# A dilated 7x7 convolution in two-dimensional point evaluation, local attention and group whitening on one core: interpolating column points in pairs, evaluating the last row point by column points, and whitening in 64x64 parts

## The chip, the core and the metric

The kernel runs on one core of one Trainium2 chip. The metric is the device time of one launch in microseconds; the figure for a kernel is the median of several runs. The engines are PE (TensorE, matrix products), DVE (VectorE), ACT (ScalarE), POOL (GpSimd) and SP (SyncE, which here issues most DMAs). Matrix products go to PSUM, from where DVE or ACT take them to SBUF.

## The reference

The input is x, 4 images of 256 channels of 64 x 64 in float32. The first layer computes 49 attention maps by a 7x7 convolution with dilation 2 (256 to 128 channels), a 1x1 convolution to 49, and a softmax over the 49; the result of the layer is, at each pixel, the sum of the 49 shifted inputs weighted by these maps. The second layer whitens 4 groups of 64 channels each over all images and pixels, with five steps of a Newton iteration, and applies a gain and a shift per channel.

```
k = lax.conv_general_dilated(x, w1, window_strides=(1, 1), padding=[(6, 6), (6, 6)], rhs_dilation=(2, 2), ...) + b1
k = lax.conv_general_dilated(k, w2, ...) + b2
attn = jax.nn.softmax(k, axis=1)
shifts = jnp.stack([xp[:, :, 2*u:2*u+H, 2*v:2*v+W] for u in range(7) for v in range(7)], axis=1)
y = jnp.einsum('bkchw,bkhw->bchw', shifts, attn)
...
Sigma = EPS * I + jnp.einsum('gdm,gem->gde', xc, xc) / m
for _ in range(T_ITERS):
    P3 = jnp.einsum('gij,gjk,gkl->gil', P, P, P)
    P = 1.5 * P - 0.5 * jnp.einsum('gij,gjk->gik', P3, Sigma_N)
xn = jnp.einsum('gde,gem->gdm', P * jnp.sqrt(rTr), xc)
```

## The kernel before

**Convolution.** The two convolutions are folded into one of 256 to 49 channels at the start. It is then computed by polynomial evaluation and interpolation, in rows and in columns: of the rows of an image, row_eval makes a linear combination for each row point (0 to 5, and a point called INF); of each of those, col_eval makes one for each column point (xh). At each pair of points PE multiplies by weights that were evaluated in the same way (conv_bank, L502), for the two halves h of the columns side by side in PSUM. The column points come in three banks, (1, 2, 0), (3, 4, INF) and (5). A point has two taps, INF has one. After each bank ACT moves the products to the buffer pv (L512). When all three banks of a row point are there, col_interp turns them into that row point's values in zz, in 22 DVE instructions (L300, L303, L307), and when all row points of an image are there, row_interp turns zz into the 49 maps, in two parts of 17 and 5 instructions. The last row point of an image, 5, is treated in two parts also in col_interp. row_interp's second part and the first of the next image's operations are put in a written order on DVE (`in_order`).

**The row point INF** is not evaluated by column points before: it is one tap, and `direct` (L608) computes it as an ordinary convolution along the columns, 28 matrix products of about 496 columns, each two records in the trace. Row points 0, 4 and 5 of image 0 are direct too. `direct_inf` loads its weights (wi) from DRAM for images 1 to 3. Weights of a row point are evaluated once (`weights`), stored to DRAM (gd) and loaded for later images on SP's queue (wr).

**Attention** of an image lies between the banks of the following ones. Its steps for a quarter of an image are transposes of the maps and of the input (L926), band loads and stores (sd, band), stream transposes on DVE (L908), the weighted sums on PE (L955) whose outcome ACT brings to the slot (L974), turns back (L987) and the moments for whitening (L1008). The list `todo` holds what is due at each of eight gaps of an image; a gap comes when the costs of the banks so far (6, 5 and 2 per row point, 12 for the direct INF) reach the next eighth. The scheduler then orders each engine's instructions; before the first bank of image 1 (`strict`) and in `in_order` blocks DVE's order is the written one.

**Whitening.** At the end each 128 x 128 matrix wm (two groups of 64 on its diagonal) multiplies slots of 512 columns (L1276), and ACT (L1287) and DVE (L1291) by turns scale and shift the product into out, which goes to DRAM in stores of 512 KB with four buffers.

## Time and profile before

| what | us |
|---|---|
| median of 3 runs | 766.35 (765.34 to 767.47) |
| profiled execution, its own time | 765.48 |
| its span in the profile | 763.7 |
| PE busy | 716.1 (94%) |
| DVE busy | 623.9 (82%) |
| ACT busy | 325.9 (43%) |
| POOL busy | 34.2 (4%) |
| products at row and column points, L502 | 251.0 |
| direct row points, L608 | 34.8 |
| weighted sums, L955 | 154.8 |
| PE in the last 59.7 us, the apply of the whitening (L1276) | 55.02 |

The mean granted clock of PE was 0.982 of full speed. An engine's busy time sums the instructions of the profile; the span is what one execution takes from first to last instruction, and about 1.8 us of the profiled time lie outside of it. A group's line names the line of the kernel, the engine, the operation, the buffers (out from in), the shape, the count, and after the bar busy time and mean ns. Idle time ahead of an engine's instruction is put down to what ended it. One matrix product in float32 is two records.

### The profile page before, as it was taken

How to read it: one execution, taken by the hardware profiler on the slowest of the kernel's cores; microseconds unless marked ns; L12 is line 12 of the kernel's file. 1: busy time of each engine (PE TensorE's matmuls, PEld its weight loads, DVE VectorE, ACT ScalarE, POOL GpSimd, SP SyncE). 2: the span in 40 equal slices, each digit the busy share in tenths (PEclk: the TensorE clock that was granted, in tenths of full speed). 3: DMA queues.
4: the chain of work that ended last, by engine and by line, in shares of the span. 5: the costliest groups of instructions: out<-in, count | busy, mean ns of one | idle time of the engine just before them, and what ended most of it. 6: DMA issues, size and time to landing. Idle time of an engine off the chain costs nothing.

```text
span 763.7 us, 18389 instructions
## 1 busy us (share of the span) xinstructions
PE 716.1 (94%) x7444; PEld 545.6 (71%) x7444; DVE 623.9 (82%) x1302; ACT 325.9 (43%) x950; POOL 34.2 (4%) x46
## 2 busy tenths in 40 slices
PE   7999999789899999989999999998999889998997
PEld 1459643376798885979988948897998678775443
DVE  3799999999899999979995999699979665435443
ACT  2414240127544652665435435625535653332443
POOL 0510000300000010001000100000000000000000
PEclk9999999999899999999999999999999999998999
DMA  8991110054453672165545710443422143380776
GB/s 330 245 310 71 64 61 20 33 161 130 128 174 130 230 249 64 51 241 193 172 118 219 231 44 24 144 128 121 138 69 87 45 144 103 110 346 4 293 307 280
DMA packets 59773, 114.76 MB, mean 150 GB/s; under 512 B 22903, under 2 KB 42024, under 8 KB 58920
## 3 DMA queue, kind: packets, MB, share of 16 engines
q1 hardware_dynamic: 55992, 94.71, 37.1%
q0 software_dynamic: 3696, 18.88, 7.3%
q8 instruction: 59, 0.97, 0.5%
q14 instruction: 26, 0.21, 0.1%
HBM read 66.23 MB, written 47.33 MB: 149 GB/s over the span
## 4 chain that ended last, share of the span: by engine, by line
PE 41%; DVE 36%; ACT 5%; issue 4%; DMA 2%; SPq 1%; DVEq 0%; ACTq 0%
PE y L955 12%; PE cv L502 10%; PE tp L1276 7%; DVE xh L307 4%; PE sig L1008 3%; PE tp L987 3%; PE tp L926 3%; DVE rb L307 3%; DVE pv L307 3%; DVE ct L307 3%; DVE zz L307 3%; DVE band L908 2%; DVE ct L300 2%; DVE pv L303 2%; PE cv L608 2%
## 5 line engine op out<-in xcount | busy, mean ns | idle before, releaser
L502 PE MATMUL cv<-xh,wr 128*49 128x128 f32 x4368 | 251.0, 276 | 7.6 <-DVE xh L300 5.6
L502 PEld LDWEIGHTS cv<-xh,wr 128*49 128x49 f32 x4368 | 244.9, 124 | 12.7 <-issue 8.2
L955 PE MATMUL y<-band,xb 128*128 128x224 f32 (+2 forms) x640 | 154.8, 382 | 13.3 <-ACT xb L934 8.1
L955 PEld LDWEIGHTS y<-band,xb 128*128 128x128 f32 x640 | 111.8, 197 | 35.6 <-ACT xb L934 10.4
L512 ACT COPY pv<-cv 113x486 f32<-113x486 f32 (+1 forms) x63 | 29.9, 476 | 77.7 <-PE cv L502 76.6
L974 ACT ACTIVATE slot<-y,pivot 128x512 f32<-128x512 f32 x53 | 36.7, 741 | 60.5 <-PE y L955 60.5
L995 ACT COPY yt<-tp 128x256 f32<-128x256 f32 x128 | 45.4, 378 | 35.1 <-PE tp L987 34.1
L926 PE MATMUL tp<-ident,slot 128*128 128x128 f32 x256 | 50.5, 300 | 6.6 <-ACT yt L995 6.6
L987 PE MATMUL tp<-ident,slot 128*128 128x128 f32 x256 | 51.8, 298 | 3.9 <-ACT xb L934 1.4
L908 DVE STREAM_TRANSPOSE band<-band 128x960 f32<-128x960 f32 (+1 forms) x48 | 50.9, 1060 | 3.9 <-DMA band<-sd 3.8
L987 PEld LDWEIGHTS tp<-ident,slot 128*128 128x128 f32 x256 | 41.4, 205 | 13.9 <-issue 4.5
L926 PEld LDWEIGHTS tp<-ident,slot 128*128 128x128 f32 x256 | 40.1, 206 | 14.0 <-ACT yt L995 8.5
L1291 DVE TENSOR_SCALAR out<-tp,scale,beta 128x512 f32<-128x512 f32 x32 | 25.9, 810 | 29.5 <-PE tp L1276 29.5
L857 ACT COPY zt<-d 32x112 f32<-32x112 f32 (+2 forms) x156 | 45.0, 288 | 1.7
L811 ACT ACTIVATE d<-tp,mx 128x49 f32<-128x49 f32 x128 | 37.0, 337 | 14.5 <-DVE mx L806 10.8
L1287 ACT ACTIVATE out<-tp,beta,scale 128x512 f32<-128x512 f32 x32 | 24.9, 777 | 32.0 <-PE tp L1276 32.0
L307 DVE SCALAR_TENSOR_TENSOR xh<-ct 128x512 f32<-128x512 f32 x42 | 27.8, 683 | 12.4 <-PE cv L502 12.2
L934 ACT COPY xb<-tp 128x256 f32<-128x256 f32 x87 | 30.5, 380 | 16.6 <-PE tp L926 16.0
L1008 PE MATMUL sig<-yt 128*64 128x65 f32 x1024 | 36.9, 225 | 0.0
L1008 PEld LDWEIGHTS sig<-yt 128*64 128x64 f32 x1024 | 32.5, 137 | 6.0 <-issue 4.5
L1276 PE MATMUL tp<-slot,PS 128*128 128x512 f32 x80 | 35.9, 593 | 0.0
L608 PE MATMUL cv<-slot,wi 128*49 128x496 f32 (+3 forms) x168 | 34.8, 571 | 0.0
(206 smaller groups left out, 985.6 us busy)
## 6 DMA issues: line engine op xcount, KB each, us to landing
out_dram<-out SPq DMA_DIRECT2D x32, 512.0 KB, 2.6
sd<-zt SPq DMA_DIRECT2D x16, 896.0 KB, 3.9
slot<-in_x_dram POOLq DMA_DIRECT2D x12, 1024.0 KB, 10.3
band<-sd SPq DMA_DIRECT2D x128, 84.0 KB, 2.1
wr<-gd SPq DMA_DIRECT2D x15, 588.0 KB, 4.0
wr<-gd SPq DMA_DIRECT2D x15, 490.0 KB, 3.5
spill<-slot POOLq DMA_DIRECT2D x3, 2048.0 KB, 8.2
back<-spill SPq DMA_DIRECT2D x3, 2048.0 KB, 8.0
```

The lines of the kernel that those rows point to most:

```text
L307: return in_turn(STT(o, a, f, b, ALU.mult, ALU.add))
L502: nc.tensor.matmul(cv[h * HB : h * HB + KT, k, sr : sr + n, sc : sc + n], wv[:, sc, sr, cc], xh[bc][:, :n, h * NCC + cc, :n], start=(j == ...
L608: nc.tensor.matmul(ps[h * HB : h * HB + KT, :, w0:w1_], w[v][:, cc], xs[:, :, cc, w0 + d : w1_ + d], start=(j == 0), stop=(j == len(order) ...
L811: nc.scalar.activation(d[:, h, i], lt[i // NI][:, i % NI, h, :KT], AF.Exp, bias=mx[:, i, h : h + 1], accum_out=s[:, h, i : i + 1],)
L857: ins = nc.scalar.copy(o, i)
L908: nc.vector.transpose(f, f)
L926: nc.tensor.transpose(t[:, cc * P : (cc + 1) * P], xt[:, cc, CR * m : CR * (m + 1), bass.ds(pc, SW, 2)], ident,)
L955: nc.tensor.matmul(ps[:, cc, q0 - half * HALF : q1 - half * HALF, :], xb[:, cc * P : (cc + 1) * P], rhs, start=(k == 0), stop=(k == len(PI ...
L987: nc.tensor.transpose(t[:, cc * P : (cc + 1) * P], yt[:, cc, CR * i : CR * (i + 1), bass.ds(pc, SW, 2)], ident,)
L995: nc.scalar.copy(yb.rearrange("p a g c -> p (a g) c")[:, :, :GW], t[:, :C].rearrange("p (e c) -> p e c", c=GW),)
L1008: nc.tensor.matmul(sig[g * GW : (g + 1) * GW, cc], yb[:, cc, g, :GW], yb[:, cc, g], start=(count[0] == 0 and cc == 0), stop=(count[0] == 4 ...
L1276: nc.tensor.matmul(t, wm[cc], slots[2 * b + pr][:, cc, q * TR : (q + 1) * TR, :].rearrange("p r w -> p (r w)"), start=True, stop=True,)
```

## The change

**Row point INF at column points.** ROWS now begins with INF, and images 2 and 3 have seven row points, all of them evaluated at column points; INF's weights have one tap and are half as wide (98 for 196). They are made from a kept copy in DRAM (kept[INF]) at image 2 and loaded at image 3. Image 0's INF stays direct; image 1's also stays direct, but moves from behind that image's first row point to the end of the written prologue. The tile wi, its load and direct_inf go, and so do the two zi buffers, whose place zz has now (one plane more).

**Pairs.** col_interp takes two row points at once, (INF, 0), (1, 2) and (3, 4), in instructions of 113 x 324 in place of 113 x 162; pv is one tensor with three places for row points. Where the two places aren't neighbours in order (distance -2), two of the instructions are split. Row point 5, row point 0 of image 1 and row point 3 of image 0 stay single. The sum that part 1 needs goes to a plane of the products, no longer to a temporary.

**Prologue and costs.** The prologue's order changes with the pairs, and a bank's cost is scaled by its taps; there is no step of 12 for INF.

**Whitening.** The apply takes two blocks q of 512 columns together. For the first of the two column parities each is a product of 128 x 128 as before; the second parity is four of 64 x 64, two that write the partitions of their own group and two that write those of the other (ts[1]). The exchanged ones are brought back by two 64-partition moves, with scale and shift exchanged too (abx, made by one more product with a swap matrix). Products of 64 x 64 alternate between a pair of banks of ps_y and cv_buf; out has six buffers.

```
...
-ROWS = (0, 1, 2, 3, 4, 5)
+ROWS = (INF, 0, 1, 2, 3, 4, 5)
+PAIRS = ((INF, 0), (1, 2), (3, 4))
+AT = {br: k for k, br in enumerate(ROWS)}
...
-    zz = apool.tile([P, NP - 1, Q9, W], F32, name="zz")
-    zi = [apool.tile([P, Q9, W], F32, name=f"zi{k}") for k in range(2)]
-    for k in range(2):
-        nc.gpsimd.memset(zi[k], 0.0)
+    zz = apool.tile([P, NP, Q9, W], F32, name="zz")
+    nc.gpsimd.memset(zz[:, AT[INF]], 0.0)
+    NV = 3
+    pv = apool.tile([P, NP, NV, Q9, 2 * Q9], F32, name="pv")
...
-    it = ct.rearrange("p a b -> p (a b)")[:, :PT].rearrange("p (q b) -> p q b", q=Q9)
...
-    gd = [dram.tile([P, nsl, NSK], F32, name=f"gd{b}") for b in range(NP - 1)]
+    gd = [
+        dram.tile([P, nsl, NSK * len(taps(b)) // 2], F32, name=f"gd{b}") for b in range(NP)
+    ]
...
+    kept[INF] = dram.tile([P, KS * NSK // 2], F32, name="gi")
+    nc.sync.dma_start(kept[INF], tap[:, UPOS[3]].rearrange("p v a k -> p (v a k)"))
...
-        wt = apool.tile([P, ns, NSK], F32, tag=f"wr{i}", name=f"wr_{b}_{br}_{i}")
+        nk = NSK * len(taps(br)) // 2
+        wt = apool.tile([P, ns, NSK], F32, tag=f"wr{i}", name=f"wr_{b}_{br}_{i}")[:, :, :nk]
...
-            f = rb[0].rearrange("p q r c w -> p (q r c w)")[:, : KS * NSK]
+            f = rb[0].rearrange("p q r c w -> p (q r c w)")[:, : KS * nk]
...
-            f = f.rearrange("p (v a r k) -> p v a r k", v=KS, a=NCC, r=2)
+            f = f.rearrange("p (v a r k) -> p v a r k", v=KS, a=NCC, k=KT)
...
-            ct.rearrange("p a b -> p (a b)")[:, k * NSK : (k + 1) * NSK] for k in range(3)
+            ct.rearrange("p a b -> p (a b)")[:, k * nk : (k + 1) * nk] for k in range(3)
...
                 nc.scalar.copy(r[2], xs[:, 0])
+            elif br == INF:
+                nc.scalar.copy(r[1], xs[:, 3])
             for cc in range(NCC):
...
-        return rb[{1: 2, 2: 0, 3: 0, 4: 1, 5: 2, 0: 2}[br]]
+        return rb[{1: 2, 2: 0, 3: 0, 4: 1, 5: 2, 0: 2, INF: 1}[br]]
...
-    pvs = {}
+    slot = {}
...
-            pvs[b, br] = apool.tile(
-                [P, NP, Q9, 2 * Q9], F32, tag="pv", name=f"pv_{b}_{br}", bufs=2
-            )
+            slot[b, br] = len(slot) % NV
...
             nc.scalar.copy(
-                pvs[b, br][:K2, i0 : i0 + len(pts)].rearrange("p n q b -> p (n q b)"),
-                cv[:K2, : len(pts)].rearrange("p n q b two -> p (n q b two)"),
-            )
-    def interpolate(pt, tmp, outs, cut, part=None):
+                pv[:K2, i0 : i0 + len(pts), slot[b, br]].rearrange("p n q b -> p n (q b)"),
+                cv[:K2, : len(pts)].rearrange("p n q b two -> p n (q b two)"),
+            )
+    def interpolate(pt, tmp, outs, cut, part=None, each=lambda *a: (a,)):
...
             madd(tmp, s2, -16.0, tmp)
-            add(tmp, tmp, s4)
-            madd(outs[0], lo(s1), 1.0 / 6, hi(c0))
+            for o, x, y in each(outs[0], lo(s1), hi(c0)):
+                madd(o, x, 1.0 / 6, y)
             add(outs[2], lo(c6), hi(s3))
+            add(s3, tmp, s4)
         if part != 0:
-            madd(hh, tmp, -1.0 / 9, hh)
+            madd(hh, s3, -1.0 / 9, hh)
             madd(s4, hh, -3.0, s4)
...
             madd(s2, s4, -1.0 / 15, s2)
-            madd(outs[1], lo(s4), 1.0 / 15, hi(s2))
+            for o, x, y in each(outs[1], lo(s4), hi(s2)):
+                madd(o, x, 1.0 / 15, y)
     def phases(t):
-        return [t[:, :, bass.ds(4 + a - R if a < R else 0, Q8, 4)] for a in range(4)]
+        return [t[..., bass.ds(4 + a - R if a < R else 0, Q8, 4), :] for a in range(4)]
     def col_interp(b, br, part=None):
-        pv = pvs[b, br]
-        pt = {c: pv[:K2, i] for i, c in enumerate(ORDER)}
-        outs = phases(zz[:K2, br].rearrange("p q (w two) -> p q w two", two=2))
...
-        interpolate(pt, t[:K2], outs, cut, part)
+        brs = br if isinstance(br, tuple) else (br,)
+        s0, ds = slot[b, brs[0]], slot[b, brs[-1]] - slot[b, brs[0]]
+        v = pv[:K2, :, s0]
+        v = bass.AP(
+            tensor=v.tensor,
+            offset=v.offset,
+            ap=[list(v.ap[0]), [NV * PT, NP], [ds * PT, len(brs)], [2 * Q9, Q9], [1, 2 * Q9]],
+        )
+        pt = {c: v[:, i] for i, c in enumerate(ORDER)}
+        z = zz[:K2, AT[brs[0]] : AT[brs[0]] + len(brs)]
+        outs = phases(z.rearrange("p n q (w two) -> p n q w two", two=2))
+        cut = lambda t, k: t[:, :, :, 2 * k : 2 * (k + Q8)].rearrange(
+            "p n q (b two) -> p n q b two", two=2
+        )
+        t = ct.rearrange("p a b -> p (a b)")[:, : len(brs) * PT].rearrange(
+            "p (n q b) -> p n q b", q=Q9, n=len(brs)
+        )
+        each = lambda *a: (a,)
+        if ds not in (0, 1):
+            each = lambda *a: [[t[:, k] for t in a] for k in range(len(brs))]
+        interpolate(pt, t[:K2], outs, cut, part, each)
         if part != 0:
             nc.scalar.copy(outs[3], cut(pt[5], 0))
+        if INF in brs:
+            nc.gpsimd.memset(zz[:, AT[INF], Q8], 0.0)
     def row_interp(b, part):
-        pt = {k: zz[:K2, k] for k in range(NP - 1)}
-        pt[INF] = zi[b % 2][:K2]
+        pt = {k: zz[:K2, AT[k]] for k in range(NP)}
         lg = lgx
...
         lg = lg[:, : SH * W].rearrange("p (r w) -> p r w", w=W)
-        outs = [t[:, 0] for t in phases(lg[:K2].unsqueeze(1))]
+        outs = phases(lg[:K2])
         cut = lambda t, k: t[:, k : k + Q8]
-        tr = zi[(b + 1) % 2]
+        tr = ct.rearrange("p a b -> p (a b)")[:K2, : Q9 * W].rearrange("p (q w) -> p q w", w=W)
+        interpolate(pt, tr, outs, cut, part)
         if part == 0:
-            interpolate(pt, tr[:K2], outs, cut, 0)
             done_ = ((0, outs[0]), (2, outs[2]))
         else:
-            interpolate(pt, tr[:K2], outs, cut, 1)
-            nc.gpsimd.memset(tr[:, Q8], 0.0)
             done_ = ((3, cut(pt[5], 0)), (1, outs[1]))
...
-        z = zi[b % 2][:K2] if br == INF else zz[:K2, br]
+        z = zz[:K2, AT[br]]
...
-    gi = dram.tile([P, KS, NCC * KT], F32, name="gi")
-    nc.sync.dma_start(gi, tap[:, UPOS[3]].rearrange("p v a k -> p v (a k)"))
...
-    def direct_inf(b):
-        t = apool.tile([P, KS, NCC, KT], F32, tag="wi", name=f"wi_{b}")
-        nc.sync.dma_start(t.rearrange("p v a k -> p (v a k)"), gi.rearrange("p v k -> p (v k)"))
-        w = [t[:, v] for v in range(KS)]
-        direct(b, INF, 0, conv_psum(), w)
...
-    rows += [(b, br) for b in range(1, B) for br in ROWS]
+    rows += [(b, br) for b in range(1, B) for br in ROWS[1 if b == 1 else 0 :]]
...
-            if b > 0 and br == ROWS[-2]:
-                with in_order():
-                    col_interp(b, br)
-                    row_interp(b, 0)
-            else:
+            if b == 1 and br == 0:
...
+            for p in PAIRS:
+                if br == p[1] and (b, p[0]) in slot:
+                    last = br == ROWS[-2]
+                    with in_order() if last else nullcontext():
+                        col_interp(b, p)
+                        if last:
+                            row_interp(b, 0)
...
-        if br in kept:
+        if br in xrs:
...
-    nxt.update(weights(0, 3, 0))
-    col_eval(xr, 0)
-    direct0(0, 1)
-    nxt.update(weights(0, 3, 1))
-    col_eval(xr, 1)
-    nxt.update(weights(0, 3, 2))
+    for i in three:
+        nxt.update(weights(0, 3, i))
+        col_eval(xr, i)
+        if i == 0:
+            direct0(0, 1)
+    for i in three:
+        bank(2, i)
...
-    col_interp(0, 1)
-    col_eval(xr, 2)
-    bank(2, 0)
-    bank(2, 1)
...
-    bank(2, 2)
...
     row_eval(0, 5, [rb[0], rb[1], xrs[5]])
-    col_interp(0, 2)
+    col_interp(0, (1, 2))
     direct0(4, 1)
+    direct0(5, 0)
     col_interp(0, 3)
     row_interp(0, 0)
-    direct0(5, 0)
-    for i in three:
-        prepare(NR0, i)
+    prepare(NR0, 0)
     direct0(5, 1)
     row_interp(0, 1)
+    direct(1, INF, 0, acc[:, 0], [tap[:, UPOS[3], v] for v in range(KS)])
+    prepare(NR0, 1)
+    prepare(NR0, 2)
     strict[0] = False
...
         steps = []
-        for r in range(len(ROWS)):
-            k = NR0 + len(ROWS) * (b - 1) + r
-            for i, cost in enumerate((6, 5, 2)):
-                steps.append((cost, lambda k=k, i=i: conv_step(k, i)))
-        inf = (12, lambda b=b: direct_inf(b))
+        for k, (bk, br) in enumerate(rows):
+            if bk == b:
+                for i, cost in enumerate((6, 5, 2)):
+                    steps.append(
+                        (cost * len(taps(br)) / 2, lambda k=k, i=i: conv_step(k, i))
+                    )
         if b == 1:
-            steps[:3] = [
-                *steps[:3], (0, lambda: soft(0, 0)), inf, (0, lambda: soft(0, 1)),
-            ]
-        else:
-            steps.insert(0, inf)
+            steps.insert(0, (0, lambda: soft(0, 0)))
+            steps.insert(4, (0, lambda: soft(0, 1)))
         j, at, whole = 0, 0, sum(c for c, _ in steps)
...
     rpool = ctx.enter_context(tc.tile_pool(name="rp", bufs=1, reuse_waits="tile"))
+    swap = rpool.tile([P, P], F32, name="swap")
+    for g in range(P // GW):
+        nc.gpsimd.tensor_copy(
+            swap[:, g * GW : (g + 1) * GW], ident[:, (1 - g) * GW : (2 - g) * GW]
+        )
     blk = rpool.tile([P, P], F32, name="blk")
...
-    wm, sc, beta = {}, {}, {}
+    wm, sc, beta, abx = {}, {}, {}, {}
...
-        scale = work.tile([P, 1], F32, tag="scale", name=f"scale{cc}")
+        ab = work.tile([P, 2], F32, tag="ab", name=f"ab{cc}")
+        scale = ab[:, 0:1]
...
-        bt = work.tile([P, 1], F32, tag="beta", name=f"beta{cc}")
+        bt = ab[:, 1:2]
...
+        yield
+        t = tp()
+        nc.tensor.matmul(t[:, :2], swap, ab, start=True, stop=True)
+        abx[cc] = work.tile([P, 2], F32, tag="abx", name=f"abx{cc}")
+        nc.vector.tensor_copy(abx[cc], t[:, :2])
...
     NT = 512
     TR = NT // W
-    n = 0
+    n = [0]
+    def out_rows(o, i, scale, bias):
+        n[0] += 1
+        if n[0] % 2:
+            nc.scalar.activation(o, i, AF.Identity, bias=bias, scale=scale)
+        else:
+            nc.vector.tensor_scalar(o, i, scale, bias, ALU.mult, ALU.add)
+    def two_banks():
+        while True:
+            t = ps_y.tile([P, 2, NT], F32, tag="y", name="apply")
+            yield [t[:, k] for k in range(2)]
+            yield cv_buf
+    G0, G1 = slice(0, GW), slice(GW, P)
+    two = two_banks()
     for b in (3, 2, 1, 0):
         for cc in range(NCC):
-            for q in range(SH // TR):
-                st = rpool.tile([P, TR, 2, W], F32, tag="out", name=f"out_{b}_{cc}_{q}", bufs=4)
-                for pr in range(2):
+            for q in range(0, SH // TR, 2):
+                st = [
+                    rpool.tile([P, TR, 2, W], F32, tag="out", name=f"out_{b}_{cc}_{q + k}", bufs=6)
+                    for k in range(2)
+                ]
...
+                ts = next(two)
+                def plain(k):
                     t = tp()
+                    pe(nc.tensor.matmul(t, wm[cc], y[0][k], start=True, stop=True))
+                    out_rows(st[k][:, :, 0, :], rows_of(t), sc[cc], beta[cc])
...
+                plain(0)
+                for k in range(2):
+                    for i in (G0, G1):
+                        o = i if k == 0 else (G1 if i is G0 else G0)
+                        pe(
+                            nc.tensor.matmul(
+                                ts[k][o], wm[cc][i, i], y[1][k][i],
+                                start=True, stop=True, skip_group_check=True,
+                            )
+                        )
+                out_rows(st[0][:, :, 1, :], rows_of(ts[0]), sc[cc], beta[cc])
+                store(0)
+                for i, o in ((G1, G0), (G0, G1)):
+                    out_rows(
+                        st[1][o][:, :, 1, :], rows_of(ts[1])[i], abx[cc][i, 0:1], abx[cc][i, 1:2]
+                    )
+                plain(1)
+                store(1)
 # ---- launch: one core; inputs and outputs as the reference has them ----
...
```

## The prediction

> **What bounds the kernel now.** I read the page's busy times first, then its slices, its chain by engine, the groups, and last the PE timeline and windows around each stage that the diff touches.
>
> ```profile
> span 763.7 us, 18389 instructions
> PE 716.1 (94%) x7444; PEld 545.6 (71%) x7444; DVE 623.9 (82%) x1302; ACT 325.9 (43%) x950; POOL 34.2 (4%) x46
> PE   7999999789899999989999999998999889998997
> DVE  3799999999899999979995999699979665435443
> PE 41%; DVE 36%; ACT 5%; issue 4%; DMA 2%; SPq 1%; DVEq 0%; ACTq 0%
> ```
>
> PE has 47.6 us of idle time in the whole span, DVE 139.8. But DVE's slack isn't spread evenly: up to slice 28 it is at nine tenths nearly everywhere, and the slack lies in the last quarter. The chain splits itself almost evenly. So in the first three quarters any PE work that is removed was also cover for DVE, and removing it pays only if DVE can feed the next bank in time.
>
> ```profile
> 150.81 8.21 PE L502 MATMUL cv<-xh,wr 128*49 128x128 f32 x96 [5.59 <-DVE xh L300]
> 203.43 11.80 PE L502 MATMUL cv<-xh,wr 128*49 128x128 f32 x208
> 294.14 11.59 PE L608 MATMUL cv<-slot,wi 128*49 128x512 f32 x56
> 449.02 11.59 PE L608 MATMUL cv<-slot,wi 128*49 128x512 f32 x56
> 703.84 27.71 PE L1276 MATMUL tp<-slot,PS 128*128 128x512 f32 x64
> ...
> 294.00:305.70 11.70, 11.70 (x59) 3.62 (x58) 11.39 (x30) 1.78 (x5) 0.00 (x0) 1.00 0.08 23
> 449.00:460.50 11.50, 11.50 (x57) 3.56 (x56) 11.40 (x18) 2.22 (x5) 0.15 (x1) 1.00 0.07 20
> 704.00:763.70 59.70, 55.02 (x128) 24.06 (x128) 26.32 (x35) 24.86 (x32) 0.00 (x0) 1.00 0.69 281
> ```
>
> Timeline lines give start, length, group and, in brackets, the idle time ahead and who ended it. Window lines give PE, PEld, DVE, ACT, POOL busy, then clock, DMA share and GB/s. One row point costs PE 11.80 us for 208 records, 57 ns a record; a direct INF costs 11.59 us. In both INF windows DVE is busy 11.4 us of 11.5 to 11.7: PE needs nothing from DVE there (slots and stored weights only), and DVE uses the time to finish the old image and prepare the new one.
>
> ```profile
> L307 DVE SCALAR_TENSOR_TENSOR pv<-pv 113x162 f32<-113x162 f32 x105 | 33.7, 321 | 1.0
> L307 DVE SCALAR_TENSOR_TENSOR zz<-zz 113x576 f32<-113x576 f32 x16 | 12.1, 756 | 0.4
> ...
> L1291 DVE TENSOR_SCALAR out<-tp,scale,beta 128x512 f32<-128x512 f32 x32 | 25.9, 810 | 29.5 <-PE tp L1276 29.5
> L1287 ACT ACTIVATE out<-tp,beta,scale 128x512 f32<-128x512 f32 x32 | 24.9, 777 | 32.0 <-PE tp L1276 32.0
> ```
>
> In the groups, the two columns after the bar are busy time and mean ns; the last tells whom the engine waited for. The column and row interpolations (L307) give DVE's price for two sizes; the evictions of the apply wait for PE, not the other way about.
>
> **The skill.** "TensorE: Matmul & The Clock Gate", Part 1, says that an idle window of about 3.4 us halves PE's clock. The first line above agrees in kind: after 5.59 us idle, 96 records took 8.21 us, not 96 x 57 ns = 5.5. Part 3 of that page says that matmuls on different row and column groups run at once (9 small ones 6.32 times faster). The trace shows columns alone: 57 ns for 128 columns is 0.45 ns a column, where a full apply record takes 55.05 / 128 = 430 ns for 512, 0.84 a column. No row packing occurs before. "TensorEngine Tiling (Array Packing)" says, under Key Properties, that a change of tiling mode drains PE, and under Gotcha 1 that two row tiles cannot use one PSUM bank at a time; nothing before shows either.
>
> **The parts.** Sums are against the profiled execution, 765.48 us (span 763.7 plus 1.8); the median is 0.9 above it, so I add the sum to 766.35.
>
> *Pairs.* The group rows give 321 ns for 162 elements and 756 for 576: 1.05 ns an element and 151 ns fixed. A pair's 113x324 should take 491, so 22 of them 10.4 us (with small ones) against two single interpolations, of which one ran from 119.78 to 126.57, 6.79 us: 3.2 us of DVE less a pair. One pair pays in image 0, two in image 1. In images 2 and 3 the third pair contains INF, which is new work. What it is worth is set by whether DVE is late for the next xh. Where PE has its xh, it is worth nothing, and the cover is a row point's 11.8 us of PE against 6.84 of evaluation. A row point's interpolation now waits for its partner; three pv slots in place of two buffers allow that, so ACT's eviction of the third row point doesn't wait. Part 1 of the interpolations without a temporary is the same number of instructions: nothing.
>
> *INF at column points, images 2 and 3.* PE: one tap, 104 records of 57 ns = 6.0 us in banks of 2.8, 2.3 and 0.9, for 11.6: -5.6 each, if fed. DVE: +6.84 (the column evaluation of a row point, summed from its timeline) - 2.8 (each of the three pairs saves 3.2, the INF column interpolation itself adds 6.79), +4 an image; image 2 also makes the INF weights, 20 instructions of about 254 ns = 5.1 us. Both are the small cost; the order below is the large one. SP gets one load of the kept weights and three stores of the made ones in image 2, and in image 3 three half-size loads in place of the single load of the direct weights. They stand in SP's queue among the wr and band loads; a whole wr load (588 KB) lands in 4.0 us by the page and is issued one row point, 11.8 us, ahead. I take nothing; a late one would cost its 4 us.
>
> Is it fed? The instruction order of the changed kernel puts on PE: row 5's banks, the last attention turn, INF banks 0, 1, 2, row 0 bank 0, and only then attention (two of its steps, 7.9 us, stood beside the direct INF before). On DVE, between INF's xh for bank 0 and for bank 1 of image 2, stand the first part of row 5's col_interp 6.5 us, weights 1.8, two band transposes 2.0, row_interp part 1 4.2 and ct, xh 2.3: 16.8 us. PE covers 2.8, and stalls 14.0. Weights and xh of bank 2 take 5.0, PE covers 2.3: 2.7 more. So 6.0 + 16.7 for 11.6: **+11**. Behind the waiting matmul stand all attention turns, and ACT's evictions. A stall of 14 us also costs clock, about 2.7 us as at 150.81: **+2.5**.
> Image 3 makes no weights, and its order is kinder: before bank 1 come 20 instructions of col_interp (6.2), a transpose (1.2) and the evaluation (2.3), 9.7 less PE's 2.8 and about 1 us lead: 5.9; before bank 2 the rest of col_interp, row_interp part 1 and xh, 7.9 less 2.3: 5.6. 6.0 + 11.5 - 11.6: **+6**, clock **+1.5**.
> From the other side: if nothing waited, each image would gain 5.6; if row 0 were late as well, each would lose some 5 more.
>
> *Recovery.* While PE is stalled, DVE and ACT get ahead. PE's later waits within images 2 and 3, all on ACT's turns, are 5.9 and 5.5 us; I give back a third: **-4** (0 to -11). At the end of image 3 the pair (3,4) is 3.6 us longer than a single one with about 3 us of slack: **+1**.
>
> *Prologue.* The order there is fixed. DVE's chain from 93 to 165 us gets 3.1 us shorter by the one pair. The direct INF of image 1 (11.6 us, needs nothing of DVE) moves into PE's 5.59 us wait, so row 0 of image 1 is fed; but the INF no longer stands in image 1, where it covered DVE's work for its second row, whose xh now comes after three band transposes (L908): PE waits some 8 us there and the clock goes cold. **-1** (-4 to +3). Image 1's lower costs run banks a little ahead of attention; nothing.
>
> *Tail.* Before, a pair of q takes 4 passes of 0.86 us (55.05 / 64); after, three, if four 64x64 matmuls share a pass: 16 x 3 x 0.86 = 41.3 us, -13.8. Evictions become 5 a pair, 80 in all, 40 an engine at the rows' 0.78 to 0.81 = 32 us: hidden under 41, not below it. The stores are 32 x 512 KB = 16.8 MB; at the window's 281 GB/s for a share of 0.69 full queues would give about 405, the best slice of the page is 346: 41 to 48 us. With drains I take 47 for 55: -8, and the extra swap matmul, copy and DVE's beta ahead of the first apply cost 1.3: **-7** (-12.5 to +5; the upper end if the 64x64 ones run one after another or two by two with drains).
>
> Sum: 11 + 2.5 + 6 + 1.5 - 4 + 1 - 1 - 7 = +10, so 766.35 + 10: **776 us**.
>
> **Rivals.** *PE stays fed (faster).* The stalls depend on how DVE's queue drains: if PE arrives at INF bank 0 some 14 us later than I place it (DVE 3.2 us lighter a pair, attention longer), banks 1 and 2 find xh ready and the ledger counts: -5.6 x 2 - 1 - 7 = -19, 747 us. For it: 139.8 us of DVE idle. Against: DVE busy 11.39 of 11.70 just there. It decides at total stalls under about 9 us of my 28; half of that way gives 757.
> *Packing fails (slower).* Row tiles of one bank serialize, or switches eat the pass: the tail gives +1 in place of -7, 783 us, up to 790. For it: no such matmul before. Against: the skill's figure.
> *Cancelling.* Recovery takes 11 and the tail 10: 765.
>
> **How the numbers follow.** The measurement tells 0.3%, 2.3 us, from no change. Stalls with a working tail 0.50 (own range 769 to 782); fed 0.21 (741 to 763); packing fails 0.18 (781 to 790); cancelling 0.11 (763 to 769), of which 0.08 is within the bound. Faster 0.22, same 0.09, slower 0.69. From 757 to 788 leaves out the best half of the fed case and the worst of the packing one.
>
> **What will show it.** PE waits on DVE's xh of 14 and 3 us ahead of the second and third INF bank of image 2, and about 6 twice in image 3; 104 records for each INF; pair instructions at 0.49 us; 41 to 48 us of apply, at 340 GB/s or more. Wrong if those waits are under 4 us, if the apply stage stays at 55, or if the second row of image 1 delays PE by more than 10 us.

## The result, and the profile after

The changed kernel takes 788.44 us (786.47 to 792.80, 4 runs) against 766.91 (765.34 to 767.82): 1.0291 times the time before, with an interval of 1.0243 to 1.0339. It is 21.5 us slower. The forecast was 776 with a range up to 788. Here and below a ratio is to the kernel before on the same chip, over fast runs alone, with its 95% interval in brackets. Where the intervals of two kernels overlap much, a difference between their medians is not clear of noise.

From the page of the changed kernel: span, busy times, the slices of PE and DVE, the chain by engine, and the group of the products at row and column points (after the bar: busy time, mean ns, idle time ahead of the group on PE and its main releaser).

```profile
span 784.7 us, 18660 instructions
PE 704.8 (90%) x7608; PEld 543.8 (69%) x7608; DVE 642.1 (82%) x1200; ACT 343.6 (44%) x971; POOL 33.7 (4%) x45
PE   6999989984999985999999877999899889998997
DVE  2899999998998989999963999999759956554665
PE 46%; DVE 29%; DMA 5%; ACT 4%; issue 3%; SPq 1%; DVEq 0%; ACTq 0%
L513 PE MATMUL cv<-xh,wr 128*49 128x128 f32 (+1 forms) x4576 | 272.9, 282 | 32.2 <-ACT pv L523 12.5
```

PE is busy 11.3 us less and idle 32.3 us more: 79.9 for 47.6. The change takes about 19 us of work from PE (5.6 for each INF row, 8 in the tail), but the products at points now take 59.6 ns a record (272.9 us for 4576) where they took 57.5, which puts some 10 us back: PE's mean granted clock is 0.964 for 0.982. Of the new idle time 24.6 stands ahead of this one group (32.2 for 7.6). Counted from 0, the slices show three new dents in PE, with DVE at eight or nine tenths beside them. Slice 9 is a wait of 9.9 us ahead of image 1's second row point, shown below. Slices 15 and 23 to 24 are the two places where an image ends and INF's row point of the next begins.

The PE timeline there (start, length, group, in brackets idle time ahead and its releaser), and the windows around it (busy PE, PEld, DVE, ACT, POOL, then clock, DMA share, GB/s):

```profile
298.50 2.87 PE L513 MATMUL cv<-xh,wr 128*49 128x128 f32 x48
311.08 4.15 PE L513 MATMUL cv<-xh,wr 128*49 128x128 f32 x40 [9.72 <-ACT lgx L616]
316.26 6.42 PE L513 MATMUL cv<-xh,wr 128*49 128x128 f32 x112 [1.02 <-DVE xh L313]
...
462.95 2.87 PE L513 MATMUL cv<-xh,wr 128*49 128x128 f32 x48
470.71 4.53 PE L513 MATMUL cv<-xh,wr 128*49 128x128 f32 x40 [4.89 <-DVE xh L313]
479.21 7.67 PE L513 MATMUL cv<-xh,wr 128*49 128x128 f32 x112 [3.96 <-issue]
...
298.00:328.00 30.00, 19.26 (x234) 17.69 (x234) 29.59 (x60) 8.98 (x22) 0.00 (x0) 0.83 0.33 88
462.00:488.00 26.00, 17.14 (x223) 15.87 (x220) 25.31 (x46) 6.71 (x15) 0.00 (x0) 0.80 0.24 66
```

An INF row point has 104 records: 48, 40 and 16, the last together with the first 96 of row point 0. The first bank goes through; the second waits 9.7 us in image 2 and 4.9 in image 3; the third 1.0 and 4.0. Both second banks run at a cold clock (40 records in 4.15 and 4.53 us, where 57 ns a record give 2.3). DVE is busy 29.59 us of 30 and 25.31 of 26 there: it isn't waiting for anything, it is what PE waits for. The 9.72 are put down to ACT, but ACT's own part of that bank's xh had long been done, and DVE's first instruction of it (0.68 us) ends just before PE starts at 311.08:

```profile
295.39 0.72 ACT L485 COPY xh<-rb 128x512 f32<-128x512 f32 x1
310.26 1.28 DVE L313 SCALAR_TENSOR_TENSOR xh<-ct 128x512 f32<-128x512 f32 x2
```

For the 3.96 the profile names no releaser; there too DVE's last xh for the bank, which starts at 478.42 and takes 0.68, ends about 0.1 us before PE starts.

To see where the loss arises I compare the two traces at equal PE work: at the start of the same step of the moments (sig), less the 96 records (5.44 us) of row point 0 that the changed kernel has already done at two of the marks.

| mark | before | changed | later by |
|---|---|---|---|
| image 1's row points all done | 292.39 | 296.74 | 4.35 |
| INF of image 2 done, and the attention step after it | 311.87 | 329.43 - 5.44 | 12.1 |
| image 2's row points all done | 447.26 | 461.20 | 13.9 |
| INF of image 3 done, and the attention step after it | 466.46 | 493.47 - 5.44 | 21.6 |
| last moments | 687.21 | 715.16 | 27.95 |
| end of the span | 763.7 | 784.7 | 21.0 |

The two INF rows take 7.8 and 7.6 us more than the direct ones, the stretch between them gives nothing back (1.8 more), image 3 loses 6.4, and the tail wins 6.95. The kernel with the old tail, further below, is the same program as the changed one up to the whitening; its trace repeats these stages within 2.7 us, so smaller differences between two traces say little.

The tail does what it is meant to. Its timeline in the changed kernel, 8 records being four 64x64 products:

```profile
745.48 1.99 PE L1339 MATMUL tp<-slot,PS 128*128 128x512 f32 x4
747.39 1.09 PE L1355 MATMUL cv<-slot,PS 64*64 64x512 f32 x8
748.41 1.98 PE L1339 MATMUL tp<-slot,PS 128*128 128x512 f32 x4
750.33 1.09 PE L1355 MATMUL apply<-slot,PS 64*64 64x512 f32 x8
```

From 745.48 to 748.41 is one pair of q, 2.93 us, where four whole products took 3.44. The four small ones take 1.02 us (747.39 to 748.41) against 0.86 for one whole product: nearly all the packing there can be. Times 16 this is 47 us.

### The profile page after: what moved, and what is told of

Same layout as the page of the kernel before. It is cut to its first block, busy times and chain, and to the rows that moved or that the text cites. A ratio compares the mean times of both kernels' runs of the same rounds, so it can differ in the third digit from the quotient of the medians.

```text
span 784.7 us, 18660 instructions
## 1 busy us (share of the span) xinstructions
PE 704.8 (90%) x7608; PEld 543.8 (69%) x7608; DVE 642.1 (82%) x1200; ACT 343.6 (44%) x971; POOL 33.7 (4%) x45
## 4 chain that ended last, share of the span: by engine, by line
PE 46%; DVE 29%; DMA 5%; ACT 4%; issue 3%; SPq 1%; DVEq 0%; ACTq 0%
PE cv L513 14%; PE y L973 12%; DMA band<-sd 4%; PE tp L1339 4%; DVE xh L313 3%; DVE ct L313 3%; PE tp L1005 3%; PE acc L634 3%; PE tp L944 3%; PE sig L1026 3%; DVE pv L313 2%; DVE zz L313 2%; DVE band L926 2%; DVE ct L306 2%; DVE rb L306 2%
## 5 line engine op out<-in xcount | busy, mean ns | idle before, releaser
L513 PE MATMUL cv<-xh,wr 128*49 128x128 f32 (+1 forms) x4576 | 272.9, 282 | 32.2 <-ACT pv L523 12.5
L513 PEld LDWEIGHTS cv<-xh,wr 128*49 128x49 f32 x4576 | 264.7, 127 | 38.3 <-issue 16.2
L973 PE MATMUL y<-band,xb 128*128 128x224 f32 (+2 forms) x640 | 153.0, 378 | 19.4 <-ACT xb L952 17.0
L523 ACT COPY pv<-cv 113x486 f32<-113x486 f32 (+1 forms) x69 | 32.8, 478 | 109.2 <-PE cv L513 82.6
L926 DVE STREAM_TRANSPOSE band<-band 128x960 f32<-128x960 f32 (+1 forms) x48 | 50.9, 1060 | 13.4 <-DMA band<-sd 13.3
L1005 PEld LDWEIGHTS tp<-ident,slot 128*128 128x128 f32 x256 | 41.3, 205 | 13.4 <-issue 3.8
L829 ACT ACTIVATE d<-tp,mx 128x49 f32<-128x49 f32 x128 | 37.2, 328 | 15.4 <-DVE mx L824 13.3
L313 DVE SCALAR_TENSOR_TENSOR xh<-ct 128x512 f32<-128x512 f32 x46 | 30.1, 683 | 15.9 <-PE cv L513 15.5
L313 DVE SCALAR_TENSOR_TENSOR pv<-pv 113x324 f32<-113x324 f32 (+1 forms) x84 | 36.1, 430 | 1.5
L634 PE MATMUL acc<-slot,tap 128*49 128x496 f32 (+3 forms) x168 | 34.6, 569 | 0.0
L952 DVE COPY xb<-tp 128x256 f32<-128x256 f32 x41 | 16.4, 421 | 21.5 <-PE tp L944 21.4
L306 DVE TENSOR_TENSOR ct<-rb 128x1024 f32<-128x1024 f32 (+2 forms) x32 | 30.5, 970 | 2.3 <-DMA rb<-g5d 1.5
```

What stands on the lines that cost most here:

```text
L306: return in_turn(TT(o, a, b, ALU.add))
L313: return in_turn(STT(o, a, f, b, ALU.mult, ALU.add))
L513: nc.tensor.matmul(cv[h * HB : h * HB + KT, k, sr : sr + n, sc : sc + n], wv[:, sc, sr, cc], xh[bc][:, :n, h * NCC + cc, :n], start=(j == ...
L634: nc.tensor.matmul(ps[h * HB : h * HB + KT, :, w0:w1_], w[v][:, cc], xs[:, :, cc, w0 + d : w1_ + d], start=(j == 0), stop=(j == len(order) ...
L926: nc.vector.transpose(f, f)
L952: (nc.vector.tensor_copy if tail else nc.scalar.copy)(xb, t[:, :C])
```

## The experiments

**What is asked.** Theory 1: first evictions of a row point wait for interpolations of other places in pv, which they needn't. Theory 2: the INF rows are the loss; 2a, because their small banks stand where nothing covers DVE's work for the old image; 2b, because DVE has more work, wherever it stands. Theory 3: pairs concentrate DVE's work, to a loss where no image follows.

**Plane by plane.** In the program of the changed kernel the copy of a bank covers two or three planes of pv at one place, with the other places' words in between, and 11 of these copies carry a wait for DVE. Copies of single planes do not cross the other places.

```
-            nc.scalar.copy(pv[:K2, i0 : i0 + len(pts), slot[b, br]]..., cv[:K2, : len(pts)]...)
+            for k in range(len(pts)):
+                nc.scalar.copy(pv[:K2, i0 + k, slot[b, br]]..., cv[:K2, k]...)
```

> The changed kernel with the bank's products moved to pv plane by plane (two or three copies in place of one), so that the copies to one place of pv no longer wait for an interpolation on another place. Theory 1 (the first eviction of a row point waits for the interpolation of other places, and holds the turns of attention behind it on ACT): PE's wait of 9.9 us ahead of image 1's second row point falls under 4, its waits of 3.4 to 3.8 us on the xb copies at the images' ends go, 776 to 780 us. Theory 2 (only the INF rows of images 2 and 3 cost): 787 to 790, since ACT gets 0.6 us more a row point.

Measured: 784.18 us, 1.0252 (1.0229 to 1.0276) of before. By the medians that is 4.3 us better than changed, but the intervals overlap. The waits of these copies on DVE are gone, so the theory is right in kind; the time stays above the 776 to 780 expected, so it is not the main cause. The wait ahead of image 1's second row point didn't fall either. The PE timeline after image 1's first row points, first of the changed kernel, then of this one:

```profile
196.06 10.11 PE L513 MATMUL cv<-xh,wr 128*49 128x128 f32 x128 [9.90 <-ACT pv L523]
```

```profile
197.82 7.10 PE L513 MATMUL cv<-xh,wr 128*49 128x128 f32 x96 [11.18 <-DVE xh L306]
```

The wait there changes its releaser and gets no shorter: behind the copy, xh was late as well.

**Direct INF.** The 12-cost step and direct product come back for images 2 and 3, the pair (INF, 0) goes, everything else stays.

```
-    rows += [(b, br) for b in range(1, B) for br in ROWS[1 if b == 1 else 0 :]]
+    rows += [(b, br) for b in range(1, B) for br in ROWS[1:]]
...
+        f = rb[1].rearrange("p q r c w -> p (q r c w)")[:, : KS * NCC * KT]
+        nc.sync.dma_start(f, kept[INF])
+        direct(b, INF, 0, conv_psum(), [t[:, v] for v in range(KS)])
...
+            steps.insert(0, (12, lambda b=b: direct_inf(b)))
```

> The changed kernel with INF of images 2 and 3 direct again (weights loaded to the unused row buffer rb[1]), all else as changed; row point 0 is then interpolated alone in every image. Theory 2 (the INF rows cost 7.8 and 7.6 us at the two boundaries by the two traces): 772 to 775. Theory 1 alone, with the INF rows innocent: 785 or more.

Measured: 767.12 us, 1.0008 (0.9992 to 1.0024). Undoing the INF rows gives 21.3 us, as much as the whole loss and more than the 13 to 16 that theory 2 put; the rest of the change (prologue, pairs, tail) comes to nothing in sum. The edit also takes images 2 and 3 back to six row points, which use the places of pv in another turn and put attention's gaps elsewhere, so the 21.3 is for the two INF rows with all that goes with them. The marks say where: against this kernel, the changed one loses 8.1 us at the first boundary, 7.6 at the second, and 7.4 inside image 2. There the kernel with direct INF makes good what it had lost in image 1 (5.6 us behind the kernel before at 292, 0.3 ahead at 447); the changed one doesn't.

> Both edits at once: INF of images 2 and 3 direct, and pv filled plane by plane. If theories 1 and 2 hold and add, 788 - 15 - 9 = 764, 761 to 767; if the pairs themselves are too long (10.4 us at once ahead of the row interpolation), 770 or more.

Both edits: 765.43 us, 0.9987 (0.9975 to 0.9998). By the medians the false waits are worth 1.7 us here and 4.3 with the INF rows; neither is well clear of noise.

**The tail alone**, in the kernel before.

> The kernel before with the whitening of the changed one alone (swap matrix, 64x64 parts, six out buffers). By the two traces from the first apply to the end 59.9 us against 53.0: 759 to 761. If the tail's gain came from the later start (stores of attention done), 765 or more.

Measured: 762.49 us, 0.9953 (0.9936 to 0.9970): 3.5 us, half of what was expected. From first apply to end its trace takes 55.0 us (704.44 to 759.4), 4.9 less than before; the first small products are slower (one group of them takes 680 ns a record for 614 in the changed kernel). The reverse, the old tail in the changed kernel:

> The changed kernel with the whitening of the kernel before (full 128x128 products, four out buffers, no swap). The traces from the first apply to the end say 59.9 us before, 53.0 after: 6.9 us; the kernel before with the new whitening alone gained 3.5. 794 to 796 if the tail is worth 6.9 here, 791 to 793 if it is worth the 3.5 of that run.

Measured: 793.18 us beside 763.88 for before on that chip, 1.0393 (1.0341 to 1.0445); its median is 4.7 us and its span 6.0 us longer than the changed kernel's, and its time over before is 7.8 us more. The new tail is worth some 3.5 to 8 us; between these the runs don't decide. From the last moments to the end, the twelve traces with the new tail take 69.5 to 72.5 us, the two with the old one 76.5 and 75.2.

**Cover or amount: INF second.** The same work, with row point 0 ahead of INF, so that 176 of its records and an attention step stand between the old image and INF.

```
-ROWS = (INF, 0, 1, 2, 3, 4, 5)
-PAIRS = ((INF, 0), (1, 2), (3, 4))
+ROWS = (0, INF, 1, 2, 3, 4, 5)
+PAIRS = ((0, INF), (1, 2), (3, 4))
```

> The changed kernel with one order changed: in images 2 and 3 row point 0 comes first and INF second (their pair is the same). The work on every engine is the same. Theory 2a (the INF row costs because its half-size banks stand just where DVE still interpolates the old image, with no PE work ahead of them): row 0's banks and an attention step of 7.9 us cover DVE there, PE's waits ahead of the INF banks fall from 9.7 and 1.0, and 4.9 and 4.0, to under 3 in all, 770 to 776. Theory 2b (DVE simply has too much work, 4 to 9 us more an image, wherever it stands): the wait moves to another bank and the time stays at 783 or more.

Measured: 789.64 us, 1.0306 (1.0283 to 1.0330). Theory 2a falls. Its PE timeline:

```profile
300.07 5.53 PE L513 MATMUL cv<-xh,wr 128*49 128x128 f32 x96
305.91 4.70 PE L513 MATMUL cv<-xh,wr 128*49 128x128 f32 x80 [0.31 <-DVE xh L313]
318.19 1.12 PE L815 MATMUL tp<-ident,lgx 113*128 113x113 f32 x8
319.24 6.92 PE L513 MATMUL cv<-xh,wr 128*49 128x128 f32 x120
330.90 1.82 PE L513 MATMUL cv<-xh,wr 128*49 128x128 f32 x16 [4.73 <-ACT wr L429]
335.38 8.36 PE L513 MATMUL cv<-xh,wr 128*49 128x128 f32 x96 [2.66 <-DVE xh L306]
```

Row point 0 goes through almost without a wait, and 25 us later the same time is lost: 4.7 for the last INF weights, 2.7 for the xh after them, and a cold bank (96 records in 8.36 for 5.5). At the mark where both orders have done the same work, 349.68 here and 349.89 in the changed kernel, nothing is won. Here cover put ahead only moves the wait to the next bank that DVE hasn't reached.

**DVE's amount.** Two kernels leave DVE work out; their expectations say which part.

```
+        if br == INF:
+            nc.sync.dma_start(wt, kept[INF][:, : ns * nk]...)
+            return w
...
-        col_eval(cur["x"], i)
+        if br != INF:
+            col_eval(cur["x"], i)
```

> The changed kernel with the making of INF's weights left out: in images 2 and 3 the first words of the kept INF taps are loaded as they are (20 DVE instructions, about 5.1 us, ACT's scaling and three stores gone; the maps of images 2 and 3 come out of wrong weights). Theory 2b (PE waits at the boundary of images 1 and 2 for DVE's amount of work, wherever it stands): PE's waits there lose 4 to 5 us, 781 to 785. If the waits are of another kind (the copies on ACT, PSUM), 787 or more.

Measured: 786.19 us, 1.0260 (1.0244 to 1.0276): by the medians 2.3 us less, for 5.1 us of DVE, and inside the interval of the changed kernel. It falls between the two expected ranges and decides nothing.

> The same with INF's column evaluation left out too in images 2 and 3: PE multiplies the xh that row point 5 left (the maps are wrong), so all of PE's and ACT's eviction work for the INF rows stays, and their pair's interpolation, while 6.84 us of DVE an image go. Theory 2b: the INF rows then give PE's ledger, 5.6 us an image under direct (767.1), less 3.6 us of DVE for the pair: 756 to 764. If the half-size banks cost by themselves (evictions, turns of the two PSUM buffers): 775 or more.

Measured: 772.82 us, 1.0076 (1.0048 to 1.0105). Taking away the two column evaluations, 2 x 6.84 = 13.7 us of DVE, takes 13.4 us of time from the run before it: over the whole, about one for one. The time lies between the two expected ranges, above 764 and under 775. The timeline and windows there:

```profile
300.58 6.03 PE L516 MATMUL cv<-xh,wr 128*49 128x128 f32 x104
308.48 5.53 PE L516 MATMUL cv<-xh,wr 128*49 128x128 f32 x96 [1.87 <-DVE xh L306]
...
454.76 6.04 PE L516 MATMUL cv<-xh,wr 128*49 128x128 f32 x104
465.89 7.04 PE L516 MATMUL cv<-xh,wr 128*49 128x128 f32 x96 [5.09 <-DVE xh L306]
...
298.00:328.00 30.00, 28.13 (x414) 26.21 (x414) 29.32 (x43) 14.77 (x50) 0.00 (x0) 0.99 0.26 77
```

The INF row itself now runs in 6.03 us without a wait: in this run its small banks, evictions and PSUM turns add nothing to it, so what its banks had waited for was DVE's work for the row: its evaluation, and in image 2 the weights. But even this kernel is 5.7 us slower than the one with direct INF, though PE has 11 us less to do. By the marks, its first boundary is 3.6 us shorter than with direct INF (15.6 for 19.2), so most of the 5.6 us that PE saves there does arrive. The second is 1.1 longer, after the wait of 5.09 for DVE. What is lost is lost inside image 2, which takes 8.8 us more. PE waits 9.5 us there, 3.3 with direct INF, and the longest of these waits stand behind ACT:

```profile
349.96 1.03 ACT L526 COPY pv<-cv 113x486 f32<-113x486 f32 x2 [5.24 <-DVE zz L313]
350.58 1.98 PE L516 MATMUL cv<-xh,wr 128*49 128x128 f32 x32 [2.84 <-ACT pv L526]
435.83 1.02 PE L977 MATMUL y<-band,xb 128*128 128x224 f32 x4 [2.32 <-ACT xb L956]
437.92 0.80 PE L977 MATMUL y<-band,xb 128*128 128x96 f32 x4 [1.06 <-ACT xb L956]
```

The first is an eviction that waits for the outputs of a pair at other places of pv, theory 1's wait, and the last two are what the next experiment traces to such a wait in the changed kernel. So theory 2b is shown for the evaluation, 13.4 us, and not for the 5.7 us that stay: they stand at least in part at pv. INF's part of the pair, 3.6 us of DVE an image by the prediction's prices, was not left out alone; what it costs is open.

**pv place by place.** The other way to take the false waits away, with one copy a bank as before.

```
-    pv = apool.tile([P, NP, NV, Q9, 2 * Q9], F32, name="pv")
+    pv = apool.tile([P, NV, NP, Q9, 2 * Q9], F32, name="pv")
```

> The changed kernel with pv laid out place by place, so that a bank's products are again one copy and don't touch the range of another place; every pair splits its two half-size outputs, 2 short instructions more a pair. It has the waits of the run with plane-wise copies gone without that run's extra copies on ACT. Theory 1 (size open): that run gained 4.3 us; if the extra copies hid more of it, 778 to 783; if 4 us is all, 784.

Measured: 782.21 us, 1.0223 (1.0187 to 1.0259): 6.2 us better than changed by the medians, just clear of noise. From the answers on ACT's waits, first of the changed kernel, then of this one (in total us, times, longest):

```profile
ACT pv L523 <- PE cv L513: 82.6, 36, 6.2
ACT pv L523 <- DVE zz L313: 26.1, 11, 3.3
```

```profile
ACT pv L523 <- PE cv L513: 108.5, 44, 12.2
```

How 26.1 us of an engine that is 44% busy reach PE shows at the end of image 2. ACT's and PE's timelines of the changed kernel, first ACT:

```profile
441.84 0.45 ACT L594 COPY zz<-pv 113x288 f32<-113x288 f32 x1 [3.18 <-DVE pv L313]
442.19 0.36 ACT L952 COPY xb<-tp 128x256 f32<-128x256 f32 x1
443.81 0.56 ACT L523 COPY pv<-cv 113x486 f32<-113x486 f32 x1 [1.25 <-DVE zz L313]
444.27 0.38 ACT L952 COPY xb<-tp 128x256 f32<-128x256 f32 x1
...
442.61 1.02 PE L973 MATMUL y<-band,xb 128*128 128x224 f32 x4 [2.32 <-ACT xb L952]
444.70 1.17 PE L973 MATMUL y<-band,xb 128*128 128x96 f32 x4 [1.07 <-ACT xb L952]
446.65 8.60 PE L513 MATMUL cv<-xh,wr 128*49 128x128 f32 x112
```

The copies stand in ACT's order: the pair's own copy waits for DVE, then the eviction of row point 5 waits for the pair's last output although its place is another one, and the xb copies of attention come behind both. PE waits 2.3 and 1.1 us for those, and the next 112 records take 8.60 us, cold, for 6.48. In the kernel with pv place by place the wait is 0.51 and the bank takes 6.48; it is 4.9 us ahead at the mark of image 2's end. It loses 3.6 of these at the next boundary, where DVE sets the time, and wins 5.5 more in image 3, at one wait of the same kind. The changed kernel there (ACT, then PE), and PE with pv place by place:

```profile
558.80 1.03 ACT L523 COPY pv<-cv 113x486 f32<-113x486 f32 x2 [2.55 <-DVE zz L313]
560.16 4.87 PE L973 MATMUL y<-band,xb 128*128 128x320 f32 x12 [3.84 <-ACT xb L952]
```

```profile
555.16 3.18 PE L973 MATMUL y<-band,xb 128*128 128x320 f32 x12 [0.26 <-ACT xb L952]
```

That is 3.6 us of waiting and 1.7 of clock, nearly all that image 3 had lost against before (6.4). Copies plane by plane take the same away in image 3, and nothing in image 2.

**Pairs.** The kernel with direct INF and plane-wise copies, without the pairs of images 1 to 3, and with those of image 3 alone undone, whose edit is shown.

```
+            if b in (3,) and br in (1, 2, 3, 4):
+                with in_order() if br == 4 else nullcontext():
+                    col_interp(b, br)
+                    if br == 4:
+                        row_interp(b, 0)
-            for p in PAIRS:
+            for p in PAIRS if b not in (3,) else ():
```

> The kernel with direct INF and pv filled plane by plane (765.4), with every row point of images 1 to 3 interpolated alone; the pair of image 0, the order of the prologue, the costs and the whitening stay as changed. Theory 3 (pairs gain while an image follows, and lose in the last image, where the trace loses 9 us from the middle of image 3 on): 762 to 766, near the kernel before with the new whitening alone (762.5). If the order of the prologue costs by itself, 767 or more.

> The same with pairs in images 1 and 2 and single row points in image 3. Theory 3: 757 to 761, under every kernel so far; if pairs gain nothing anywhere, 763 or more.

Measured: 767.75 us, 1.0037 (1.0018 to 1.0056) without these pairs; 761.60, 0.9968 (0.9944 to 0.9992), with pairs in images 1 and 2; 765.43 with all. By the medians pairs gain 6.2 us in images 1 and 2, clear of noise (up to image 3 the traces show 2.7 of it, 463.80 with all pairs for 466.49 without), and lose 3.8 in image 3. The loss is less sure: the two runs are from different chips, and against before on each the difference is 1.5 us with overlapping intervals. The traces speak for it: from the second boundary to the last moments image 3 takes 228.7 us with pairs and 224.4 without. It doesn't hold for every kernel, though: with INF at column points and the false waits gone, image 3 keeps its pairs and takes 221.3 and 221.7, for 220.75 before. So theory 3 fits the kernels with direct INF; why pairs cost there and not here is open.

The run with pairs in images 1 and 2 stayed just above the 757 to 761 expected. The one without pairs missed by more: it is 5.3 us above the kernel before with the new tail (762.49), where little was to be expected. By the marks it isn't the prologue: both stand at 466.49 and 466.50 before image 3's attention. They part in image 3; row buffer rb[1], which this experiment uses for INF's weights, and the plane-wise copies may be part of it. That is open.

> Direct INF, pairs in images 1 and 2, single points in image 3, pv laid out place by place in place of plane-wise copies (761.6 with these). 757 to 761 if the plane-wise copies on ACT cost in image 3; 762 if not.

Measured: 762.98 us, 0.9967 (0.9953 to 0.9981): the same as with plane-wise copies. Of all kernels, three are a little faster than before (0.995 to 0.997), none of them clearly the best; the shortest way there is the new tail alone in the kernel before.

## Why the prediction was wrong

The sign was right, and so were the waits at the INF banks; the size was not: +10 was forecast, +21.5 measured, half a microsecond outside the range. By the marks the error is almost wholly in what was to happen after the INF rows. The recovery and the end of image 3 were put at -3 together and came to +8.2, 11 us off. The prologue was 5.4 worse than put and the two boundaries 5.6 better, which cancel.

- *The INF rows.* The terms 11 + 2.5 and 6 + 1.5 make 21 us. At the boundaries themselves they came to 7.8 and 7.6, 15.4 in all. The 21.3 us by undoing them agree with the 21 by luck, since they take in 7.4 us inside image 2 that the terms don't mean. The waits are there, and smaller: 9.7 and 1.0 for 14.0 and 2.7, 4.9 and 4.0 for 5.9 and 5.6. They were argued from the place ("PE covers 2.8, and stalls 14.0"), so that another order might have mended them; INF second didn't.
- *Recovery, -4.* This is the step that failed. "While PE is stalled, DVE and ACT get ahead. PE's later waits within images 2 and 3, all on ACT's turns, are 5.9 and 5.5 us; I give back a third." Between the boundaries the changed kernel loses another 1.8 us, and in image 3 another 6.4. While PE waits for an INF bank, DVE has no free time to get ahead (29.59 us busy of 30). And PE's waits on ACT's turns didn't shrink but grew: ahead of the weighted sums those for the xb copies come to 17.0 us in the whole trace, 8.1 before. ACT was held up by waits that the prediction had put at nothing, in the next point.
- *"Three pv slots in place of two buffers allow that, so ACT's eviction of the third row point doesn't wait."* Wrong: 11 first evictions wait, 26.1 us in sum, since the places lie interleaved in pv. With pv place by place the stretch of image 2 is 4.0 us shorter than before and image 3 is 0.9 longer, close to the -4 and +1 that were put. That is one trace, and its second boundary is 3.6 us longer than the changed kernel's, so the whole gains only 6.2. The cause was to be seen beforehand: the program of the changed kernel carries these waits, and I had counted places and not asked what a copy spans.
- *Prologue, -1.* +4.35 at the end of image 1, from 9.9 us ahead of its second row point where some 8 were put. With direct INF it is made good by the end of image 2. What the prologue's order costs by itself was not tried alone.
- *The end of image 3, +1.* The pair (3, 4) was not what cost there: image 3's 6.4 us are mostly the one false wait shown above. With direct INF, undoing its pairs gave 3.8 by the medians.
- *Tail, -7.* 47 us of PE for 47 put (53.0 from the first apply to the end of the last store), 6.95 us by the traces; 3.5 by doing it alone, 4.7 to 7.8 by undoing it.
- *Pair instructions.* 491 ns was worked out, which was right: the group below, nine of its 14 being pairs, has a median of 487 (the middle of the three figures):

```profile
L309 DVE TENSOR_TENSOR pv<-ct,pv x14: 322/487/497, 116.0 to 614.8; 113x324 f32<-113x324 f32 x9, 113x162 f32<-113x162 f32 x5
```

Of the rivals, "PE stays fed" is out by the waits, "packing fails" by 1.02 us for four products (the 783 put for it should be 784 by its own terms). The time came near the upper end of the range for another reason than the one that the end was drawn for.

## What to carry to other kernels

Where a window shows two engines busy for its whole length (here PE 11.70 and DVE 11.39 us of 11.70), be wary of crediting work that is taken from one of them while work is added to the other. Here 13.7 us of DVE's work cost 13.4 us of time, so price such work one for one until a run says otherwise. Of the 5.6 us that PE saved, with that work gone, 3.6 arrived at one boundary and nothing at the other, where PE waited for DVE again. Filling the gap with other work in front moved the wait to the next bank. And before crediting a recovery later on, look at what the program makes each engine wait for there. When places of a buffer are to be independent, look at what one copy spans, not at how many places there are: interleaved places bring waits that a count of buffers hides, and on ACT these held up the copies of attention that stood behind them.

## What the runs showed of the hardware

Four float32 products of 64x64 on 512 columns take 1.02 us together, from start to start, one of 128x128 0.86. Two of them use different rows of the array and write different partitions of the same PSUM bank, and still run together; the warning of the Trainium skill ("TensorEngine Tiling (Array Packing)", Gotcha 1: PSUM Pressure) on two row tiles and one bank does not show here, and the measurement decides. A pair of q takes 2.93 us, 0.35 more than three passes of 0.86, so its two changes between tile sizes cost at most that together.

The clock also fell without one long wait. Two waits of 2.3 and 1.1 us, with a microsecond of work between them, make 3.4 us of idle time in 4.4. The granted clock (the third figure from the end) was full until the second wait and half after it:

```profile
442.00:443.70 1.70, 1.02 (x4) 0.68 (x4) 1.63 (x5) 0.55 (x2) 0.00 (x0) 1.00 0.49 115
446.65:448.00 1.35, 1.35 (x15) 1.35 (x16) 1.21 (x3) 1.35 (x4) 0.00 (x0) 0.50 0.00 0
```

The next 112 records took 77 ns each in place of 58, so 3.4 us of waiting in two pieces cost 2.1 us of clock on top. The Trainium skill ("TensorE: Matmul & The Clock Gate", Part 1) puts the half clock after at least one idle window of about 3.4 us; here no single wait was that long. How much work a window may hold and still count as idle, no run here tells.
